# Attention of a conv/attention hybrid in 64-token chunks with two heads on the partitions, softmax sums on TensorE

## Chip, cores, metric

One core of a Trainium2 chip runs the whole program. The metric is the device time of one execution in microseconds; the time before is the median of three runs. A time within 0.2% of it cannot be told from no change.

## The reference

Input x is [16, 128, 64, 64] (16 images, 128 channels, 4096 tokens each). Layer 0 is a selective-scan (Mamba-like) block with a residual; layer 1 is an attention whose score doesn't depend on a query token, and then a routed feed-forward. The change is in the attention:

```python
def _L1_attn_ref(x, W_kv, q_proj):            # x: layer-normed tokens [16, 4096, 128], 8 heads of 128
    kv = jnp.einsum('btd,ed->bte', x, W_kv).reshape(b, t, h, d, 2)
    kv = jax.nn.silu(kv)
    k, v = (kv[..., 0], kv[..., 1])
    s = jnp.einsum('hd,bthd->bth', q_proj, k)          # one score per token and head
    m_A = jax.lax.cummax(s, axis=1)                    # running maximum over the tokens
    exp_scores = jnp.exp(s - m_A)
    u_A = jnp.cumsum(exp_scores, axis=1)               # running sum
    w_A = jnp.cumsum(exp_scores[..., None] * v, axis=1)
    output = w_A / u_A[..., None]
    return output.mean(axis=2)                         # mean over the heads
```

So each token's output is a mean over heads of a weighted running sum of all values so far. Kernels before and after get exp(s) once per token, write the weight of token s in the output of token t as exp(s_s - m_s - log u_t), and keep the sum over finished chunks as a carry.

## The kernel before

The program has three parts: the fused scan and attention, the routing, and the feed-forward with its write-back. The change lies in the first, which runs from the start to about 9590 us.

Work goes in blocks of 512 tokens (`L`), 8 per image, 128 in all. The outer loop runs over k; in round k the scan works on block k (`cur`), ends block k-1 (`prev`: gate, output projection) and prepares block k+1 (`nxt`: convolution, `xproj`, `delta`), while the attention works on block k-9 (`m`), ends block k-10 (`mp_`) and norms block k-8 (`mn`). The first nine rounds have no attention, 119 have both, and the last ten have attention alone. The inner loop runs over n = 0 to 15, the states of the scan: DVE multiplies (`bx`) and scans (`h`, two halves), POOL multiplies by C (`da`), PE adds it up in `y_ps` (`add_y`, called from `sums_of_y`), and ACT makes the decays exp(delta A) eight states ahead (`decays`, each decay two activations of 128x512 written to `da`). Between these, `beside(n)` places the pieces of the attention, convolution and projections, written out by hand; `between(n)` stands between the two half scans on DVE.

All five engines run in program order: every call goes through the class `InOrder`, so in the profile these instructions all carry line 31 and are told apart by their tiles. An instruction that waits therefore holds up everything written after it on its engine; transfers are issued by SP, ACT and POOL in the same order. PSUM gives three banks in turn to nearly all products (`bank`, pool `ps`), one to `acc` (the scores `s_ps` or the attention's sums `ao_ps`), and the rest to `y_ps` and `bx`.

The attention of a block, in order:
- `ln_center` to `ln_apply`: layer norm; DVE writes `xn` at n = 14 from `rstd`, which ACT makes at n = 10.
- `key` (8 heads, n = 0 to 2): a product of 512 columns and a SiLU on ACT each (`k_ps`, `kt`).
- `score` (n = 1 and 3): 8 heads x 4 chunks of 128 tokens, weights of 32 columns, into `s_ps`, whose row 32j+5g+c holds chunk c of head 4g+j.
- `score_max`, `score_less` (n = 4), `score_exp`, `score_sum` (n = 6), with `from_chunks` for what the earlier chunks hand over: running maximum and sum by scans on DVE, exp and logarithm on ACT.
- `score_log`, `rest`, `split`, `store_parts` (n = 7), `spread_parts` (n = 10, SP): scores and logarithms are split in three bf16 parts, written to DRAM, and read back as rows of `lh` and `rh`, so that a product gives the log weights.
- `inverse` (n = 7): `e`, the factor 1/u for the carry; `turn_weights` (n = 8): exp(s) transposed into `e1`.
- `value` (n = 8, 9 for the first half, n = 3 of the next round for the second): 4 chunks x 2 products of 512 columns.
- `weights`, `attend`, `carry_on`, `attend_before`: per chunk of 128 tokens the log weights and the mask by products in `w_ps`, two exps on ACT (`wm`), 8 products of 128x128 into `ao_ps` (channel-major), 8 small ones for the carry, a copy of the carry on ACT. Chunks 0 and 1 at n = 11 to 14, chunks 2 and 3 at n = 4 to 8 of the next round.
- `add_x`, `finish`: the residual by a product with the identity, a scaled copy and a store, each for half a block.

Of the kernel before, what the change touches and what calls it, by code (L numbers as in the profile page):

```python
# [8 lines left out]
F32 = mybir.dt.float32  # L9
# [6 lines left out]
P = 128  # L16
# [23 lines left out]
def conv_attn_hybrid(ctx: ExitStack, tc: tile.TileContext, x, w_in, conv_w, conv_b, w_xproj, w_dt, b_dt,  # L40
# [6 lines left out]
    NCH = T // P  # L47
    DI = w_in.shape[1] // 2
# [32 lines left out]
    with ExitStack() as st:  # L81
# [10 lines left out]
        identb = [wp.tile([P, P], BF16, name=f"identb{u}") for u in range(2)]  # L92
        nc.vector.tensor_copy(identb[0], ident)
        for u in range(2):
            nc.vector.tensor_copy(identb[1][:, bass.ts(u, 64)], ident[:, bass.ts(1 - u, 64)])
        minusb = wp.tile([P, P], BF16, name="minusb")
        nc.vector.tensor_scalar(minusb, ident, -1.0, None, ALU.mult)
        ident_hd = wp.tile([P, P], F32, name="ident_hd")
        nc.vector.tensor_scalar(ident_hd, ident, float(HD), None, ALU.mult)

        maskb = [wp.tile([P, P], BF16, name=f"maskb{u}") for u in range(2)]
# [21 lines left out]
        q1 = wp.tile([P, 4, 2, CB, 32], F32, name="q1")  # L123
        e1 = wp.tile([P, CB * 4, 2, 32], F32, name="e1")

        lh = wp.tile([P, L], BF16, name="lh")  # L130
        rh = wp.tile([P, 4, L], BF16, name="rh")
        off = wp.tile([P, CB], F32, name="off")
        carry = wp.tile([P, L // P, P], F32, name="carry")
        negc = wp.tile([P, 1], F32, name="negc")
        zs = {what: [wp.tile([P, 32], F32, name=f"z_{what}{a}") for a in range(2)] for what in ("max", "sum")}
        for z in (*zs["max"], *zs["sum"]):
            nc.gpsimd.memset(z, 0.0)
        nc.vector.memset(negc, NEG)
        nc.vector.memset(q1, 0.0)
        nc.vector.memset(e1, 0.0)  # L140
        nc.vector.memset(carry, 0.0)
        nc.vector.memset(lh, 0.0)
        for u in range(2):
            rows = slice(64 * u, 64 * u + 64)
            nc.vector.tensor_reduce(negc[rows, :], ident[rows, 64 * u + 12 : 64 * u + 15], mybir.AxisListType.X, ALU.add)
        nc.vector.tensor_scalar(lh, lh, negc, None, ALU.subtract)
        nc.vector.memset(rh, 0.0)
        for x in range(4):
            for u in range(2):
                rows = slice(64 * u, 64 * u + 64)  # L150
                nc.vector.tensor_reduce(negc[rows, :], ident[rows, 64 * u + 3 * x : 64 * u + 3 * x + 3],
                                        mybir.AxisListType.X, ALU.add)
            nc.vector.tensor_scalar(rh[:, x, :], rh[:, x, :], negc, None, ALU.subtract)
        for c in range(CB):
            nc.vector.tensor_reduce(negc, ident.rearrange("p (j r) -> p r j", r=32)[:, c : c + 6 : 5, :],
                                    mybir.AxisListType.XY, ALU.add)
            nc.vector.tensor_scalar(off[:, c : c + 1], negc, 1.0, -OFF, ALU.subtract, ALU.mult)
# [12 lines left out]
        with tc.tile_pool(name="prep", bufs=1) as prep:  # L170
            mask = prep.tile([P, P], F32, name="mask")
            nc.gpsimd.memset(mask, 0.0)
            nc.gpsimd.affine_select(out=mask, in_=mask, compare_op=ALU.is_ge, fill=OFF, base=0,
                                    pattern=[[1, P]], channel_multiplier=-1)
            nc.vector.tensor_copy(maskb[0], mask)
            mask_ps = ps.tile([P, L], F32, tag="ps", name="mask_ps")
            nc.tensor.matmul(mask_ps[:, :P], identb[1], maskb[0], start=True, stop=True)
            nc.vector.tensor_copy(maskb[1], mask_ps[:, :P])
# [10 lines left out]
            for g in range(2):  # L189
                for c in range(CB):  # L190
                    nc.vector.tensor_copy(q1[:, :, g, c, 5 * g + c], qt_ps[:, 4 * g : 4 * g + 4])
# [18 lines left out]
        vp_ = st.enter_context(tc.tile_pool(name="vp", bufs=2))  # L210
# [278 lines left out]
        def score(m, g):  # L489
# [5 lines left out]
            for c in range(CB):  # L495
                for j in range(4):
                    PE.matmul(s["s"][32 * j : 32 * j + 32, :P], q1[:, j, g, c, :], kt[j][:, bass.ts(c, P)],
                              start=(g == 0 and c == 0), stop=(g == 1 and c == CB - 1))

        def from_chunks(m, what, local, first, op0, op1, data):  # L500

            b, i = divmod(m, NBLK)
            last = stp.tile([P, 32], F32, tag=f"last_{what}", name=f"last_{what}")
            DVE.transpose(last, local[:, P - 32 :])
            z = zs[what][m % 2]
            if i == 0:
                DVE.memset(z[:, 0:10:5], first)
            else:  # L510
                DVE.tensor_reduce(z[:, 0:10:5], gn[b][what][:, 4:14:5].unsqueeze(2), mybir.AxisListType.X, ALU.max)
            gn[b][what] = z
            for g in range(2):
                DVE.tensor_tensor_scan(z[:, 5 * g + 1 : 5 * g + 5], bc(data[:, 0:1], [P, CB]),
                                       last[:, 5 * g : 5 * g + 4], z[:, 5 * g : 5 * g + 1], op0, op1)
            back = stp.tile([P, 32], F32, tag=f"back_{what}", name=f"back_{what}")
            DVE.transpose(back, z)
            return back[:, 31:32]

# [76 lines left out]
        def value(m, c, g):  # L596
            s = att[m]
            if g == 0:
                s["v", c] = vp_.tile([P, HD, P], F32, tag="v", name="v")
# [65 lines left out]

# [556 lines left out]
```

## Time and profile before

| what | before |
|---|---|
| time of the runs | 10512.2 us median (10492.8, 10512.2, 10512.5) |
| profiled execution: span | 10498.7 us |
| profiled execution: its own time | not recorded; the span lies among the runs, 13.5 us under their median |
| fused scan and attention, last xn | 9587.7 us |
| xn to xn, a common block with scan and attention | 71.7 us |
| granted TensorE clock, mean | 0.941 |

A line of the profile names the line, the engine, the operation, the tiles as out<-in with partitions x elements, and xcount. In groups there follow the busy time, the mean ns of one, and the idle time just before with what ended it. In the timeline a line has the start and the duration in us, and merged instructions of a kind are one line with their number; in brackets stands the idle time before it with what ended it. PE's f32 products are two records each (bf16 ones and transposes one). The duration of a PE record includes the pipeline, so the cost of a group is the distance to the next group's start.

### The profile page before, as it was taken

The numbers are of one execution on the slowest core, as the hardware profiler recorded it, in microseconds if no ns is written. First come the engines' busy times: TensorE is split into PE (matmuls) and PEld (weight loads), VectorE is DVE, ScalarE is ACT, GpSimd is POOL, SyncE is SP. The second block draws the span as 40 slices with busy tenths as digits, with TensorE's granted clock in tenths as the row PEclk, the third lists the DMA queues.
The fourth block names the chain that finished last, engine by engine and source line by source line (L and its number), as shares of the span: only waits on it lengthen the run. The fifth ranks groups of instructions, "written<-read, shape, count | busy, mean of one in ns | idle before, by whom it ended". The sixth has DMA issues, their size and how long they took to land.

```text
span 10498.7 us, 163128 instructions
## 1 busy us (share of the span) xinstructions
PE 9306.2 (89%) x58461; PEld 5584.4 (53%) x58461; DVE 8947.7 (85%) x9987; ACT 7317.3 (70%) x12924; POOL 7411.9 (71%) x4387
## 2 busy tenths in 40 slices
PE   5689999999999999999999999999999999988775
PEld 3345555555555555555555555555555555545652
DVE  8999999999999999999999999999999999911743
ACT  5567777777777777777777777777777777755740
POOL 7887787878788777878787877788787878810000
PEclk7789999999999999999999999999999999998886
DMA  6676767676676667676766666676666667611358
GB/s 174 174 189 168 184 167 184 170 179 173 166 186 165 183 168 184 169 185 169 179 175 163 189 163 185 169 184 170 182 169 174 180 164 181 166 45 42 114 163 344
DMA packets 889083, 1794.65 MB, mean 171 GB/s; under 512 B 96896, under 2 KB 182544, under 8 KB 881104
## 3 DMA queue, kind: packets, MB, share of 16 engines
q1 hardware_dynamic: 732912, 1414.88, 48.0%
q0 software_dynamic: 73728, 268.47, 12.9%
q10 hardware_dynamic: 81632, 100.88, 3.0%
q8 instruction: 462, 7.57, 0.3%
q14 instruction: 349, 2.86, 0.1%
HBM read 1363.98 MB, written 151.52 MB: 144 GB/s over the span
## 4 chain that ended last, share of the span: by engine, by line
PE 46%; DVE 23%; ACT 18%; issue 9%; DMA 4%; ACTq 1%; SPq 0%; POOL 0%; DVEq 0%; POOLq 0%
DVE h L31 11%; DVE bx L31 8%; ACT da L31 7%; PE ao_ps L31 6%; PE y_ps L31 6%; PE v_ps L31 5%; PE xs_ps L31 4%; PE o_ps L31 4%; PE carry_ps L31 3%; PE k_ps L31 3%; PE dt_ps L31 2%; PE dbl_ps L31 2%; PE z_ps L31 2%; PE w_ps L31 2%; ACT wm L31 2%
## 5 line engine op out<-in xcount | busy, mean ns | idle before, releaser
L31 POOL TENSOR_TENSOR da<-h,bct 128x1024 f32<-128x1024 f32 x2048 | 6599.6, 3223 | 1718.2 <-DVE h L31 643.0
L31 DVE TENSOR_TENSOR_SCAN h<-da,state,bx 128x512 f32<-128x512 f32 x3584 | 4414.8, 1265 | 169.7 <-DVE bx L31 2.4
L31 DVE TENSOR_TENSOR bx<-du,bct 128x1024 f32<-128x1024 f32 x2048 | 2608.0, 1273 | 261.9 <-DMA bct<-bcs 195.0
L31 ACT ACTIVATE da<-delta,a_neg 128x512 f32<-128x512 f32 x4096 | 2603.0, 718 | 35.7 <-DMA da<-da 30.6
L31 PE MATMUL y_ps<-ident,da 128*128 128x128 f32 x12288 | 1773.8, 297 | 203.5 <-POOL da L31 103.8
L31 PEld LDWEIGHTS y_ps<-ident,da 128*128 128x128 f32 x12288 | 1534.0, 153 | 629.2 <-issue 372.6
L31 PE MATMUL v_ps<-wv,xn 128*128 128x512 f32 x2048 | 1031.5, 625 | 207.2 <-ACT xc L31 193.8
L31 PE MATMUL xs_ps<-xb,wc 128*128 128x512 f32 x2048 | 987.9, 620 | 141.3 <-DVE z L31 139.5
L31 PEld LDWEIGHTS ao_ps<-wm,v 128*128 128x128 f32 x8192 | 980.3, 193 | 244.2 <-issue 153.4
L31 ACT ACTIVATE v<-v_ps 128x512 f32<-128x512 f32 x1024 | 612.5, 600 | 681.6 <-PE v_ps L31 653.1
L31 PE MATMUL ao_ps<-wm,v 128*128 128x128 f32 x8192 | 1027.8, 279 | 54.7 <-ACT wm L31 45.3
L31 PE MATMUL k_ps<-xn,wk 128*128 128x512 f32 x2048 | 943.3, 594 | 0.0
L31 ACT ACTIVATE kt<-k_ps 128x512 f32<-128x512 f32 x1024 | 587.2, 600 | 207.6 <-PE k_ps L31 185.6
L31 PEld LDWEIGHTS v_ps<-wv,xn 128*128 128x128 f32 x2048 | 317.0, 188 | 758.6 <-ACT v L31 251.1
L31 ACT ACTIVATE wm<-w_ps 128x512 f32<-128x512 f32 x1024 | 555.9, 595 | 203.9 <-PE w_ps L31 197.8
L31 PEld LDWEIGHTS xs_ps<-xb,wc 128*128 128x128 f32 x2048 | 375.0, 198 | 567.4 <-issue 379.2
L31 DVE TENSOR_TENSOR_SCAN h<-da,bx 128x512 f32<-128x512 f32 x512 | 600.0, 1207 | 25.8 <-ACT w L31 0.5
L31 PEld LDWEIGHTS k_ps<-xn,wk 128*128 128x128 f32 x2048 | 370.3, 191 | 319.1 <-issue 253.1
L31 POOL COPY state<-h 128x2 f32<-128x2 f32 x1792 | 525.0, 293 | 0.0
L31 POOL DMA_DIRECT2D da<-da x512 | 449.9, 879 | 92.0 <-POOL state L31 52.6
L31 ACT ACT_TABLE_LOAD x395 | 506.8, 1283 | 9.9 <-issue 3.5
L31 ACT COPY carry<-carry_ps 128x128 f32<-128x128 f32 x512 | 133.6, 261 | 539.3 <-PE carry_ps L31 539.3
(196 smaller groups left out, 10678.1 us busy)
## 6 DMA issues: line engine op xcount, KB each, us to landing
bct<-bcs SPq DMA_DIRECT2D x2048, 512.0 KB
da<-da POOLq DMA_DIRECT2D x512, 512.0 KB, 7.8
xs<-t_d SPq DMA_DIRECT2D x240, 256.0 KB
xs<-in_x_dram SPq DMA_DIRECT2D x128, 256.0 KB
xt<-in_x_dram SPq DMA_DIRECT2D x64, 512.0 KB
t_d<-xt SPq DMA_DIRECT2D x64, 512.0 KB
t_d<-xs ACTq DMA_DIRECT2D x256, 128.0 KB
t<-t_d SPq DMA_DIRECT2D x128, 256.0 KB
```

What stands on the lines that cost most here:

```text
L31: return lambda *args, **kw: self.tc.keep_in_program_order(f(*args, **kw))
```

## The change

- Chunks have 64 tokens instead of 128, eight to a block; `s_ps` is 128 rows of 64 columns (row 32j+16g+c).
- Two heads stand on the partitions of a chunk: `value` makes the values of heads 0 to 3 on partitions 0 to 63 and of heads 4 to 7 on 64 to 127, in two products of 64 rows.
- `weights` handles four chunks in one call: one bf16 product of 94 rows and 256 columns per chunk holds log weights and mask together; 2 exps per call.
- `attend` has the weights as stationary operand: outputs are token-major (`o`, 64 tokens at a time), four products per chunk, each for two heads. The chunks' sums for the carry go to the third 128 columns of the same bank.
- `take_sums`, `carry_on`, `attend_before`: the sums are copied once per half block, and products with constant triangles (`below`, `final`) turn them into the carry before each chunk, in the bank's last 128 columns; that is copied too.
- `take_o`, `turn_o`, `finish`: the result is copied with its scale, transposed by PE into a bank of the pool `ps`, the residual added there, copied out and stored.
- The running sum isn't scanned on DVE: `turn_scores` and `score_sum` make it by products on PE (`wt`, `tri`, `below`, `final`), with the chunk's total from `score_exp`'s accumulator; only the running maximum goes over the chunks on DVE.
- `inverse` makes eight activations of 64 columns and moves from n = 7 to n = 11; `spread_scores` (for `e1`) moves to n = 6.
- `store_parts` writes rows of 64 elements, `spread_parts` issues 10 transfers instead of 16.

The diff, with the setup of constants and the old bodies (shown above) left out. The functions:

```diff
         def score(m, g):
...
             kt = [s.pop(("kt", 4 * g + j)) for j in range(4)]
+            for c in range(NC8):
+                r = 16 * g + c
                 for j in range(4):
+                    PE.matmul(s["s"][32 * j : 32 * j + 32, :64], q1[:, 4 * g + j, 31 - r : 63 - r],
+                              kt[j][:, bass.ts(c, 64)], start=(g == 0 and c == 0), stop=(g == 1 and c == NC8 - 1))
+        def score_max(m):
+            s = att[m]
+            s["mx"] = a1.tile([P, 64], F32, tag="mx", name="mx")
+            DVE.tensor_tensor_scan(s["mx"], bc(negc, [P, 64]), s["s"][:, :64], NEG, ALU.max, ALU.max)
+        def score_less(m):
+            i = m % NBLK
+            s = att[m]
+            mx, z = s.pop("mx"), zl[m % 2]
+            DVE.transpose(z[:, 32:], mx[:, 32:])
+            if i == 0:
+                DVE.memset(z[:, 0:48:47], NEG)
+            else:
+                DVE.tensor_reduce(z[:, 0:48:47], zl[1 - m % 2][:, NC8 : NC8 + 17 : 16].unsqueeze(2), mybir.AxisListType.X,
+                                  ALU.max)
+            DVE.tensor_tensor_scan(z[:, 1:25], open_, z[:, 32:56], z[:, 0:1], ALU.min, ALU.max)
+            back = stp.tile([P, 32], F32, tag="back", name="back")
+            DVE.transpose(back, z[:, :32])
+            s["x2"] = a1.tile([P, 2, 64], F32, tag="x2", name="x2")
+            DVE.scalar_tensor_tensor(s["x2"][:, 0, :], mx, back[:, 31:32], s["s"][:, :64], ALU.max, ALU.subtract)
+        def score_exp(m):
+            s = att[m]
+            s["tot"] = stp.tile([P, 1], F32, tag="tot", name="tot")
+            s["w"] = a1.tile([P, 64], F32, tag="w", name="w")
+            ACT.activation(s["w"], s["x2"][:, 0, :], AF.Exp, scale=-1.0, accum_out=s["tot"])
+        def turn_scores(m):
+            s = att[m]
+            et = s["et"] = bank("et_ps")
+            w = s.pop("w")
+            for u in range(2):
+                PE.matmul(et[64 * u : 64 * u + 64, :P], w, ident, start=True, stop=True)
+            s["wt"] = a1.tile([64, P], F32, tag="wt", name="wt")
+            ACT.copy(s["wt"], et[:64, :P])
+        def spread_scores(m):
+            et = att[m].pop("et")
+            for u in range(2):
+                rows = slice(64 * u, 64 * u + 64)
+                src = et[rows, :P].rearrange("p (j g r) -> p g r j", j=4, g=2)[:, u, :NC8, :]
+                dst = e1[rows].rearrange("p (c k) -> p c k", k=P + 1)[:, :, 16 * u : P : 32]
+                ACT.copy(dst, src)
+        def score_sum(m):
             b, i = divmod(m, NBLK)
+            s = att[m]
+            u = s["u"] = bank("u_ps")
+            PE.matmul(u[:, :64], s.pop("wt"), tri[:64, :64], start=True, stop=False)
+            PE.matmul(u[:, :64], below, bc(s.pop("tot"), [P, 64]), start=False, stop=(i == 0))
+            if i:
+                PE.matmul(u[:, :64], final[NC8 - 1], bc(gn[b].pop("sum"), [P, 64]), start=False, stop=True)
         def score_log(m):
             s = att[m]
+            u = s.pop("u")
+            ACT.activation(s["x2"][:, 1, :], u[:, :64], AF.Ln, bias=tiny)
+            last = gn[m // NBLK]["sum"] = stp.tile([P, 1], F32, tag="last", name="last")
+            ACT.copy(last, u[:, 63:64])
+            s["parts"] = a1.tile([P, 3, 2, 64], BF16, tag="parts", name="parts")
+            ACT.copy(s["parts"][:, 0], s["x2"])
         def inverse(m):
             s = att[m]
+            s["e"] = a1.tile([P, NC8, 64], F32, tag="e", name="e", bufs=2)
+            for c in range(NC8):
+                ACT.activation(s["e"][:, c], s["x2"][:, 1, :], AF.Exp, bias=off[:, c : c + 1], scale=-1.0)
...
         def store_parts(m):
             s = att[m]
+            s["pd"] = bcd.tile([3, 2, P, 64], BF16, tag="pd", name="pd")
+            ACT.dma_start(s["pd"].rearrange("t w p s -> p (t w) s"), s.pop("parts").rearrange("p t w s -> p (t w) s"))
         def spread_parts(m):
+            pd = att[m].pop("pd")
             for u in range(2):
+                for x in range(HD // 2):
+                    row, of = 64 + 12 * u + 3 * x, 32 * x + 16 * u
+                    SP.dma_start(lh[row : row + 3, :, u, :], pd[:, 0, of : of + NC8, :])
+                row = 88 + 3 * u
+                SP.dma_start(rh[row : row + 3].rearrange("t x c s -> t x (c s)"),
+                             pd[:, 1].rearrange("t (x r) s -> t x (r s)", r=32)[:, :, 16 * u * 64 : 16 * u * 64 + L])
+        def value(m, c):
+            s = att[m]
+            vp = bank("v_ps")
             for u in range(2):
+                PE.matmul(vp[64 * u : 64 * u + 64, :], s["xn"][:, bass.ts(c, 64)],
+                          wv[:, bass.ts(u, 4), :].rearrange("p h d -> p (h d)"), start=True, stop=True)
+            v = s["v", c] = vp_.tile([P, 4, P], F32, tag="v", name="v")
+            ACT.activation(v.rearrange("p x d -> p (x d)"), vp, AF.Silu)
+        def weights(m, f):
+            s = att[m]
+            wm = s["wm"] = a1.tile([P, CB, 4, 64], F32, tag="wm", name="wm", bufs=2)
+            for q in range(2):
+                rp = bank("w_ps")
+                for a in range(2):
+                    c = CB * f + 2 * q + a
+                    PE.matmul(rp[:, bass.ts(a, L // 2)].rearrange("p (x t) -> p x t", t=64),
+                              lh[:94, c].rearrange("p u s -> p (u s)"), rh[:94, :, c, :], start=True, stop=True,
+                              skip_group_check=True)
+                ACT.activation(wm[:, bass.ts(q, 2)].rearrange("p c x t -> p (c x t)"), rp, AF.Exp)
+        def attend(m, f, q):
+            s = att[m]
+            if q == 0:
+                s["o"] = acc.tile([P, 4, P], F32, tag="acc", name="ao_ps")
+            o, wm = s["o"], s["wm"]
+            v = [s.pop(("v", CB * f + 2 * q + a)) for a in range(2)]
+            for x in range(4):
+                for a in range(2):
+                    PE.matmul(o[64 * a : 64 * a + 64, q, :], wm[:, 2 * q + a, x, :], v[a][:, x, :],
+                              start=(q == 0 and x == 0), stop=False, skip_group_check=True)
+            for a in range(2):
+                c = CB * f + 2 * q + a
                 for j in range(4):
+                    PE.matmul(o[32 * j : 32 * j + 32, 2, :], e1[:, c * P + 32 * j : c * P + 32 * j + 32], v[a][:, j, :],
+                              start=False, stop=(q == 1 and a == 1), skip_group_check=True)
+        def take_sums(m):
+            s = att[m]
+            s["sums"] = a1.tile([P, P], F32, tag="sums", name="sums")
+            ACT.copy(s["sums"], s["o"][:, 2, :])
+        def carry_on(m, f):
+            b, i = divmod(m, NBLK)
+            s = att[m]
+            first = i == 0 and f == 0
+            PE.matmul(s["o"][:, 3, :], below, s.pop("sums"), start=False, stop=first, skip_group_check=True)
             if not first:
+                PE.matmul(s["o"][:, 3, :], final[NC8], gn[b]["carry"], start=False, stop=True, skip_group_check=True)
+            gn[b]["carry"] = a1.tile([P, P], F32, tag="carry", name="carry", bufs=2)
+            ACT.copy(gn[b]["carry"], s["o"][:, 3, :])
+        def attend_before(m, f):
+            s = att[m]
+            for q in range(2):
+                c = CB * f + 2 * q
+                PE.matmul(s["o"][:, q, :], s["e"][:, c : c + 2, :].rearrange("p a t -> p (a t)"), gn[m // NBLK]["carry"],
+                          start=False, stop=True, skip_group_check=True)
+        def take_o(m):
+            s = att[m]
+            s["ot"] = short("ot")
+            ACT.activation(s["ot"][:, : 2 * P], s.pop("o")[:, :2, :].rearrange("p q d -> p (q d)"), AF.Copy, scale=1.0 / HD)
+        def turn_o(m, f):
+            s = att[m]
+            s["to"] = bank("to_ps")
+            ot = s.pop("ot")
+            for q in range(2):
+                PE.matmul(s["to"][:, bass.ts(q, P)], ot[:, bass.ts(q, P)], ident, start=(q == 0), stop=False,
+                          is_transpose=True, skip_group_check=True)
+            PE.matmul(s["to"][:, : 2 * P], ident, s["x"][:, bass.ts(f, 2 * P)], start=False, stop=True,
                       skip_group_check=True)
+        def finish(m, f):
             b, i = divmod(m, NBLK)
+            s = att[m] if f == 0 else att.pop(m)
+            xs = s["x"][:, bass.ts(f, 2 * P)]
+            ACT.copy(xs, s.pop("to")[:, : 2 * P])
+            ACT.dma_start(t2_d[b, :, i * L + f * (L // 2) : i * L + (f + 1) * (L // 2)], xs)
```

Their places in the order, in `beside` (guards and unchanged pieces of other blocks cut; the `decays` lines stay):

```diff
 n == 0:
-    attend_before(mp_, 1); add_x(mp_, 0)
+    turn_o(mp_, 0)
     key(m, 0), key(m, 1), key(m, 2)
     finish(mp_, 0)
...
 n == 3:
     score(m, 1)
-    for x in range(4, 8): value(mp_, x // 2, x % 2)
+    for c in range(CB): value(mp_, CB + c)
 n == 4:
     score_max(m)
-    weights(mp_, 2)
+    weights(mp_, 1)
     conv(nxt, 0)
 n == 5:
-    attend(mp_, 2)
+    attend(mp_, 1, 0)
     score_exp(m)
     decays(k, n, 2)
-    carry_on(mp_, 2); attend_before(mp_, 2)
+    attend(mp_, 1, 1); take_sums(mp_)
 n == 6:
-    weights(mp_, 3)
+    turn_scores(m)
     out_proj(prev)
-    attend(mp_, 3)
+    carry_on(mp_, 1); score_sum(m); spread_scores(m)
     decays(k, n, 2)
     put_back(prev)
-    carry_on(mp_, 3)
 n == 7:
     score_log(m)
+    attend_before(mp_, 1)
     rest(m, 1)
+    take_o(mp_)
     split(m, 1)
     conv(nxt, 1, range(KC // 2))
     decays(k, n, 2)
     rest(m, 2); split(m, 2); store_parts(m)
-    inverse(m)
     conv(nxt, 1, range(KC // 2, KC)); conv_silu(nxt)
 n == 8:
-    attend_before(mp_, 3); add_x(mp_, 1)
+    turn_o(mp_, 1)
     finish(mp_, 1)
-    turn_weights(m); value(m, 0, 0)
+    value(m, 0)
     xproj(nxt); store_bc(nxt)
-    value(m, 0, 1)
+    value(m, 1)
 n == 9:
-    value(m, 1, 0), value(m, 1, 1)
+    value(m, 2), value(m, 3)
 n == 11:
     weights(m, 0)
+    inverse(m)
     decays(k, n, 2)
 n == 12:
-    attend(m, 0); attend_before(m, 0)
+    attend(m, 0, 0)
     decays(k, n, 2)
-    carry_on(m, 0)
 n == 13:
-    weights(m, 1)
+    attend(m, 0, 1)
     decays(k, n, 2)
+    take_sums(m)
 n == 14:
     ln_apply(mn)
-    attend(m, 1)
+    carry_on(m, 0)
     decays(k, n, 2)
-    carry_on(m, 1)
+    attend_before(m, 0)
 n == 15:
+    take_o(m)
     decays(k, n, 2)
```

In `between(n)` the call `score_less(m)` at n = 4 stays, and `score_sum(m)` at n = 6 goes.

## Prediction

> **What bounds the kernel now.** I read the busy shares of the page first:
>
> ```profile
> PE 9306.2 (89%) x58461; PEld 5584.4 (53%) x58461; DVE 8947.7 (85%) x9987; ACT 7317.3 (70%) x12924; POOL 7411.9 (71%) x4387
> PE 46%; DVE 23%; ACT 18%; issue 9%; DMA 4%; ACTq 1%; SPq 0%; POOL 0%; DVEq 0%; POOLq 0%
> ```
>
> The second line, the chain that ended last, changes engine all the time, so no busy share decides alone. I took one block (512 tokens) out of the steady stretch and read DVE in the timeline:
>
> ```profile
> 3000.21 0.69 DVE L31 TENSOR_TENSOR xn<-cen_ps,rstd 128x512 f32<-128x512 f32 x1 [1.27 <-ACT rstd L31]
> 3026.21 0.41 DVE L31 TENSOR_TENSOR_SCAN mx<-negc,s_ps 128x128 f32<-128x128 f32 x1
> 3031.32 0.68 DVE L31 TENSOR_TENSOR z<-yb_ps,z 128x512 f32<-128x512 f32 x1
> 3071.94 0.69 DVE L31 TENSOR_TENSOR xn<-cen_ps,rstd 128x512 f32<-128x512 f32 x1 [1.28 <-ACT rstd L31]
> ```
>
> From xn to xn is 71.7 us; that is the common period, and over the steady blocks the mean is 72.3. I cut it in two. Stage A runs from xn to the end of the second gate (z, 3032.0): 31.8 us, DVE without a gap. Stage B runs from there to the next xn: 39.9 us, which ends in a wait for rstd, so PE and ACT set it. How near ACT and PE are to setting stage A too is seen in their timelines:
>
> ```profile
> 3000.82 1.09 ACT L31 ACTIVATE wm<-w_ps 128x512 f32<-128x512 f32 x2 [0.65 <-PE w_ps L31]
> 3001.79 5.01 ACT L31 ACTIVATE da<-delta,a_neg 128x512 f32<-128x512 f32 x8
> 3006.70 0.25 ACT L31 COPY carry<-carry_ps 128x128 f32<-128x128 f32 x1
> 3006.84 1.08 ACT L31 ACTIVATE wm<-w_ps 128x512 f32<-128x512 f32 x2
> 3007.81 3.79 ACT L31 ACTIVATE da<-delta,a_neg 128x512 f32<-128x512 f32 x6
> 3013.00 1.28 ACT L31 ACT_TABLE_LOAD   x1
> 3014.30 1.09 ACT L31 ACTIVATE kt<-k_ps 128x512 f32<-128x512 f32 x2
> 3052.68 1.28 ACT L31 ACTIVATE e<-x,off 128x128 f32<-128x128 f32 x4 [0.41 <-ACT parts L31]
> ```
>
> ```profile
> 3003.53 0.65 PE L31 MATMUL carry_ps<-v,e 128*32 128x128 f32 x16
> 3012.82 2.74 PE L31 MATMUL k_ps<-xn,wk 128*128 128x512 f32 x6
> 3018.08 1.08 PE L31 MATMUL s_ps<-kt,q 128*32 128x128 f32 x32
> 3032.06 3.70 PE L31 MATMUL xs_ps<-xb,wc 128*128 128x512 f32 x8 [1.37 <-DVE z L31]
> ```
>
> ACT has no gap from wm to the first kt (3000.8 to 14.3). The last score product ends at 3025.45, and DVE takes it (mx) at 3026.21: stage A has 0.76 us to spare. PE waits 1.37 us for the gate before the convolution. A change that lengthens the scores' way by more than 0.8 us moves the period.
>
> **Work removed and added, per block.** DVE loses the sum's scan, two transposes, two 4-step scans and a reduce ((144.3+27.1+27.1+46.0+12.9)/128 = 2.0 us) and 0.3 on halved ones: 2.3 of 67.4 busy. PE: the weights' product drops from 5.3 ((295.9+219.2+159.9)/128) to about 1. The weighted sums have as many records, but 64 columns wide, two side by side. The nearest row, pl (128*64), issues 16 records in 1.03 us where ao needs 1.87, so 8.0 falls to 4.1. The values become 32 records of half width instead of 16. If the halves share the array as pl's do, they cost the same; if not, 16 x 0.43 = 6.9 more. I take the first plus 0.1 per lone call (0 to 0.43, a lag of one record). The scores have 128 records of 64 columns instead of 64 of 128: 16 records of this width took 0.58 us (3003.53 to the next product at 3004.11), 32 took 1.01 (3018.08 to 3019.09), so 27 ns a record and 0.15 for the group. If time followed columns, a score call would stay at 1.0; if records set it, 64 x 27 + 150 ns = 1.9. I take 1.9, since the record of M=32 also brings its own weight load. New small products (turned scores, sums, turned outputs) add 2, rest loses 0.5. PE loses some 5 us in all, and ACT comes out even: four wm of 0.49 go, and half-size exps of e (8 for 4), two take_o of 0.35, two copies and an accumulator read come.
>
> The Trainium skill (TensorE: Matmul & The Clock Gate, "Wait — 56ns, not 53.3ns?") has a rule against halving the columns: starts of products never come closer than about 25 ns however few columns they have. By it a score call is 64 x 25 ns + 150 = 1.75 us, an estimate from that page, and the sum below would be 0.3 us a block smaller.
>
> **Where it lies: stage A, T = 0 at the end of rstd (3000.17).** ACT now has inverse in front of the decays: four e of 128 columns took 1.28, so 0.32 each; da of 512 takes 0.61, hence 0.76 ns a column and 0.27 for 64 columns, 8 x 0.27 = 2.15 (half of 0.32 would make 1.3). So: wm until 1.4, inverse 3.55, then 12 da of 0.613 (n = 11 to 13) 10.9, and only then take_sums 11.1, since ACT keeps program order. PE has done both attends by about 6 and waits some 5 us in carry_on; queued behind it are y, attend_before, turn_o and the keys. carry_on (4 records of 0.117) and hand-offs 11.75, ACT's carry copy 12.1, two da 13.3, take_o 13.7, two da 14.95, table 16.25, kt0 16.85 (before: 14.7). turn_o holds one of three banks until finish, which comes after three kt, so the third key waits for kt0 and ends at 17.75; after one y the fourth key starts at 18.6, before at 16.1 (3016.27): +2.5. Two score calls add 0.9 each. The last score ends at 29.6 instead of 25.3, and mx starts at 29.7 instead of 26.04. From there to the second gate's end DVE needs 5.5 (5.79 less the halved work): stage A ends at 35.2 instead of 31.8, **+3.4**. What PE saved is spent waiting for ACT.
>
> **Stage B, t = 0 at the gate's end.** Convolution 3.55, y 4.4, both attends (2 x 1.6) 7.6, turn_scores 0.35, out_proj 3.5: 11.45 (before 12.7). PE's carry_on stands behind out_proj, and ACT's carry copy waits for it with spread_scores, four da, put_back and the logarithm queued behind; before, those da lay beside out_proj. So carry_on 11.9, copy 12.25, spread 12.65, da 15.1, put_back 16.15, Ln, last and parts 17.05, take_o and split 17.7, da 20.15, split and DMA issue 20.9, table 22.2, xc 22.9; before 23.9. e has gone from here (-1.3), but the logarithm comes later than before. From xc to rstd, PE's row of v, dbl, z and dt stays at 16.0, plus 0.3 for the halves. **-0.7**.
>
> What stays at nothing: DVE's 2.3 us, because it then waits at mx and at xn; if stage A were DVE's again, 0.3 of it would count there. spread_parts issues 10 DMAs instead of 16 on SP (0.33 us apart, -2.0), so the bct loads behind it come earlier. That shortens bx's wait for bct, which already lies ahead of the longer wait for rstd. store_parts now writes 768 rows of 128 B: its queue's mean is 3.0% x 10499 x 16 / 81632 = 62 ns a packet, so 768/16 x 62 ns = 3 us at most later, while in another block spread_parts ends at 5160.6 and the first reader starts at 5169.99. If that cover failed, the 3 us would go on stage B. The setup's extra memsets and copies are some 5 us.
>
> **The clock.** Where PE had idled 1.38 us before the convolution, the granted clock was 0.72 in one block (5128 to 5134), and its 8 records took 5.23 us to the next product instead of 3.54 at clock 1.00; about a third of the blocks have a stage B of 41.4 to 41.8 for 39.7. The new 5 us idle will meet this more often; what runs cold first has slack towards kt0. I take +0.5 a block, bounds 0 and 2. The same page of the skill ("What's actually happening") states half rate after an idle window of about 3.4 us and full rate after as long a busy one; by it the first 3.4 us after the idle would cost up to 1.7 us a block, an estimate, 200 us in all.
>
> **Sum.** 119 blocks have scans and attention: (3.4 - 0.7) x 119 = +321; clock +60. The last ten have attention alone at about 47 us each (PE-bound, without the decays that delay ACT): PE's saving of 5 less new hand-offs, -4 x 10 = -40 (0 to -60). Together +341 on the span of 10498.7. Around the span lie 13.5 us if the profiled execution was like the median, 10512.2, of runs from 10492.8 to 10512.5. That makes 10853, rounded to **10850 us**.
>
> **Rivals.** *Cost follows columns* (faster): if 64-column instructions cost half of 128-column ones, the scores add nothing (-1.8) and inverse is 1.3 (-0.85). A is then +0.75, and Ln, parts and splits take 0.4 off B, now -1.1: (0.75 - 1.1) x 119 - 40 = -82, so 10430. Records overlap four deep in s_ps now, which speaks for it; the row of 224 ns for a 64-column ACT copy against 261 for 128 speaks against. It decides once they cost less than about 65%. If ACT's order also held PE less than walked and DVE ended A again at 31.5, it would be (-0.3 - 1.1) x 119 - 40 = -207, 10305. Chance 0.24. *No change*: the added and the saved cancel within 0.2%, 21 us, about what a measurement of this kernel can tell: 0.06. *Halves don't share* (slower still): values +6.9, half in each stage, on PE's chain: 10850 + 821 = 11670; pl speaks against: 0.04. The forecast, own range 10600 to 11150: 0.66.
>
> **Numbers.** The range 10290 to 11150 leaves out about 1 in 10 on either side. Faster 0.24, same 0.06, slower 0.70.
>
> **What would show it.** Right: DVE waits at mx for s_ps; PE's longest wait in a block is carry_on's on sums; the first kt comes 16 to 17 us after rstd; a score group lasts about 1.9 us; xn to xn is about 74.5 us. Wrong: mx doesn't wait and the period is under 71.7, a score group lasts 1 us, or v_ps records don't overlap.

## The result, and the profile after

| | before | after |
|---|---|---|
| time of the runs, median | 10512.35 us (10492.82 to 10518.95) | 10687.16 us (10675.27 to 10696.04) |
| ratio, 95% interval | | 1.017 [1.0155, 1.0184] |
| profiled execution: span | 10498.7 us | 10694.3 us (its own time 10696.04) |
| mean granted TensorE clock | 0.941 | 0.908 |
| first xn / last xn | 617.2 / 9587.7 us | 620.9 / 9789.4 us |
| stage A, mean (median) of the steady blocks | 31.74 (31.80) us | 35.45 (35.44) us |
| stage B, mean (median) | 40.55 (39.75) us | 38.91 (38.35) us |
| xn to xn, mean (median) | 72.29 (71.63) us | 74.35 (74.20) us |
| xn to xn in the last blocks, attention alone | 46.8 us | 41.3 us |

The steady blocks are 109 of the 119 with scan and attention. Slower by 174.8 us, where +338 was forecast: the sign and the stage were right, the size was twice too large. The sum closes on the profiled spans: (74.35 - 72.29) x 119 = +245, ten last blocks at 41.3 instead of 46.8 = -55, and +3.7 before the first xn, together +194; the spans differ by 195.6.

Busy shares, the chain that ended last, and two groups of the page after (busy us, mean ns of one; then the idle time ahead of them and what ended it):

```profile
PE 9085.2 (85%) x68316; PEld 5489.8 (51%) x68316; DVE 8651.8 (81%) x9089; ACT 7241.1 (68%) x13564; POOL 7371.6 (69%) x4412
PE 58%; ACT 26%; DVE 9%; issue 3%; DMA 3%; ACTq 0%; POOL 0%; SPq 0%; DVEq 0%; POOLq 0%
L31 PE MATMUL ao_ps<-sums,below 128*128 128x128 f32 x512 | 135.2, 351 | 465.9 <-ACT sums L31 465.8
L31 ACT ACTIVATE kt<-k_ps 128x512 f32<-128x512 f32 x1024 | 600.8, 601 | 470.1 <-PE k_ps L31 460.3
```

Every engine is busy for less time than before, and yet the program is longer: DVE has lost 296 us and fallen from 23% of the chain to 9%, PE and ACT carry 84% of it. The two groups show how they hold each other up: PE stands 466 us before `carry_on`, waiting for ACT's copy of the sums, and ACT stands 460 us before the keys' SiLU, waiting for PE.

DVE in one block (timeline: start, duration, and in brackets the idle time ahead):

```profile
3068.95 0.69 DVE L31 TENSOR_TENSOR xn<-cen_ps,rstd 128x512 f32<-128x512 f32 x1 [3.90 <-ACT rstd L31]
3099.42 0.29 DVE L31 TENSOR_TENSOR_SCAN mx<-negc,s_ps 128x64 f32<-128x64 f32 x1 [1.68 <-PE s_ps L31]
3104.40 0.68 DVE L31 TENSOR_TENSOR z<-yb_ps,z 128x512 f32<-128x512 f32 x1
3143.43 0.69 DVE L31 TENSOR_TENSOR xn<-cen_ps,rstd 128x512 f32<-128x512 f32 x1 [1.66 <-ACT rstd L31]
```

The wait that was forecast is there: `mx` now waits for `s_ps`, and stage A (here 3068.95 to 3105.08, 36.1 us; 35.45 in the mean) is no longer DVE's. (The block shown is the first of an image, so the two records that carry the sums on from the block before are missing in it.) Who sets it can be read off the chain of waits in the same window (start, duration, what; count):

```profile
3070.09 2.01 ACT e L31 x8
3072.10 7.35 ACT da L31 x12
3079.45 0.16 ACT sums L31
3079.66 0.81 PE ao_ps L31 x2
3080.49 0.28 ACT carry L31
3080.81 1.22 PE ao_ps L31 x4
3082.03 3.41 PE y_ps L31 x16
3085.44 1.23 PE to_ps L31 x4
3086.68 2.67 PE k_ps L31 x6
3098.32 1.07 PE s_ps L31 x64
3099.42 0.06 DVE mx L31
```

Up to `sums` it is the walk of the prediction: inverse (2.01 us), twelve decays, then the copy, while PE waits. After `carry` it isn't: PE gets through 16 records of y in 3.41 us, 16 for which it needed 1.75 in a block of before:

```profile
3010.41 1.91 PE L31 MATMUL y_ps<-ident,da 128*128 128x128 f32 x16
3012.16 0.39 PE L31 MATMUL ao_ps<-e,carry 128*128 128x128 f32 x2
```

The same stretch of the kernel after in the table by windows says why (stretch and its length; busy us and count of PE, PEld, DVE, ACT, POOL; granted clock; DMA share; GB/s):

```profile
3074.50:3079.60 5.10, 1.15 (x15) 0.86 (x8) 4.93 (x5) 5.10 (x10) 3.73 (x3) 1.00 0.52 90
3079.60:3081.80 2.20, 1.79 (x6) 1.49 (x7) 2.17 (x3) 1.32 (x4) 1.87 (x3) 0.52 0.08 29
3081.80:3085.20 3.40, 3.40 (x18) 3.40 (x17) 3.27 (x3) 3.08 (x5) 3.40 (x2) 0.50 0.70 143
3085.20:3086.60 1.40, 1.40 (x7) 1.22 (x6) 1.37 (x2) 0.00 (x0) 1.08 (x2) 0.54 0.25 75
3086.60:3090.00 3.40, 3.40 (x15) 1.74 (x14) 3.23 (x4) 1.81 (x4) 3.23 (x4) 1.00 0.45 137
```

PE is idle for 4.0 us of the first row; then the clock is granted at half for some 7 us, all of it on the path to the first key. In the third row PE is busy for the whole stretch, and a reader who looks at busy shares alone takes it for the bound.

### The profile page after: what moved, and what is told of

Read it like the earlier page. It is cut to its first block, busy times and chain, and to the rows that moved or that the text cites. A ratio compares the mean times of both kernels' runs of the same rounds, so it can differ in the third digit from the quotient of the medians.

```text
span 10694.3 us, 180670 instructions
## 1 busy us (share of the span) xinstructions
PE 9085.2 (85%) x68316; PEld 5489.8 (51%) x68316; DVE 8651.8 (81%) x9089; ACT 7241.1 (68%) x13564; POOL 7371.6 (69%) x4412
## 4 chain that ended last, share of the span: by engine, by line
PE 58%; ACT 26%; DVE 9%; issue 3%; DMA 3%; ACTq 0%; POOL 0%; SPq 0%; DVEq 0%; POOLq 0%
ACT da L31 13%; PE y_ps L31 11%; PE k_ps L31 8%; PE ao_ps L31 7%; PE v_ps L31 5%; PE xs_ps L31 5%; PE o_ps L31 4%; DVE h L31 4%; PE s_ps L31 3%; ACT e L31 3%; PE dt_ps L31 3%; DVE bx L31 2%; PE z_ps L31 2%; PE dbl_ps L31 2%; ACT L31 1%
## 5 line engine op out<-in xcount | busy, mean ns | idle before, releaser
L31 DVE TENSOR_TENSOR bx<-du,bct 128x1024 f32<-128x1024 f32 x2048 | 2555.5, 1248 | 152.5 <-DMA bct<-bcs 82.7
L31 PE MATMUL y_ps<-ident,da 128*128 128x128 f32 x12288 | 1991.3, 321 | 202.9 <-DMA da<-da 101.8
L31 PEld LDWEIGHTS y_ps<-ident,da 128*128 128x128 f32 x12288 | 1760.2, 169 | 600.3 <-issue 324.7
L31 PE MATMUL v_ps<-wv,xn 128*64 128x512 f32 x4096 | 1092.2, 607 | 26.8 <-ACT xc L31 26.3
L31 PE MATMUL ao_ps<-v,wm 128*64 128x128 f32 x8192 | 573.6, 283 | 27.2 <-ACT wm L31 27.2
L31 PEld LDWEIGHTS v_ps<-wv,xn 128*64 128x64 f32 x4096 | 259.3, 135 | 575.9 <-ACT v L31 174.6
L31 PE MATMUL ao_ps<-sums,below 128*128 128x128 f32 x512 | 135.2, 351 | 465.9 <-ACT sums L31 465.8
L31 PEld LDWEIGHTS ao_ps<-v,wm 128*64 128x64 f32 x8192 | 447.9, 139 | 122.5 <-issue 52.2
L31 DVE TENSOR_TENSOR xn<-cen_ps,rstd 128x512 f32<-128x512 f32 x128 | 88.5, 691 | 507.5 <-ACT rstd L31 472.9
L31 ACT COPY carry<-ao_ps 128x128 f32<-128x128 f32 x256 | 68.2, 266 | 576.8 <-PE ao_ps L31 576.8
```

The source lines that it names most:

```text
L31: return lambda *args, **kw: self.tc.keep_in_program_order(f(*args, **kw))
```

## The experiments

Two theories were open. *Cold clock*: stage A is late because PE idles before `carry_on` and then runs at half speed. *Order alone*: it is late by ACT's queue and by PE's dependent steps, and the clock matters little, as the prediction had it (+0.5 us a block). All ratios are against the kernel before; the kernel after stands at 1.017.

**e1, the sums ahead of two decays.** ACT's copy of the sums moves in front of one `decays` call.

```diff
 n == 13:
     attend(m, 0, 1)
-    decays(k, n, 2)
     take_sums(m)
+    decays(k, n, 2)
```

> The changed kernel with take_sums(m) moved in front of the two decays of n = 13. Theory 'ACT's order and the clock': take_sums comes 2.45 us earlier, carry_on with it; the one idle stretch of PE of about 4 us is cut in two (the carry copy still stands behind the decays), PE keeps its full clock, the first kt is ACT's at 16 us after rstd instead of PE's at 18.6. Stage A falls by about 2, so 119 x 2 = 240 us less than the changed kernel: ratio to the kernel before about 0.994 instead of 1.017. Rival 'more and smaller records load PE': the order on ACT doesn't matter, ratio stays at 1.015 to 1.019. Rival 'ACT's work sets stage A': ACT has as much to do as ever, ratio 1.010 or more.

Measured: 10532.21 us, 1.0023 [1.0013, 1.0032]. `sums` comes at 7.83 us after xn instead of 10.44, the first key at 16.75 instead of 17.92, stage A is 34.25. One line moved is worth 155 us, less than the 240 expected: the clock record of its trace still has half rate in stage A of all 109 steady blocks, for 3.4 us in 73 of them and for 6.8 us in 36. That PE's wait for ACT sets the stage is shown; the two theories are not parted, since a shorter wait is also a warmer clock (in the kernel after, 56 blocks have 3.4 us and 53 have 6.8).

**e2, inverse back at n = 7.** Undoes that one move of the change.

```diff
 n == 7:
     store_parts(m)
+    inverse(m)
 n == 11:
     weights(m, 0)
-    inverse(m)
```

> The changed kernel with inverse(m) moved back from n = 11 to n = 7, behind store_parts. Theory 'ACT's order and the clock': the eight e (2.0 us) leave the front of stage A, the sums come 2.0 us earlier, PE idles 2 us less and keeps its clock for most of the time; stage A falls by 2.5 to 3.5, stage B grows by up to 2.0 as the e stand before the convolution's table load. Net -0.5 to -1.5 a block, ratio 1.000 to 1.011, with A under 33.5 and B about 40. Rival 'more and smaller records load PE': no change of A, B +2.0, ratio 1.035 or more.

Measured: 10819.17 us, 1.0295 [1.028, 1.0311]: slower than the kernel after, and outside what was expected. Stage A fell nearly as walked (35.45 to 33.08), but stage B rose by 3.4 (38.91 to 42.29). `e` itself takes 2.0 us in front of `xc`. The rest is in the timeline and the windows of PE:

```profile
3080.74 1.45 PE L31 MATMUL v_ps<-wv,xn 128*64 128x512 f32 x4 [2.29 <-ACT xc L31]
3081.97 2.77 PE L31 MATMUL dbl_ps<-xc,wx 128*40 128x512 f32 x3
```

```profile
3080.70:3082.70 2.00, 1.96 (x5) 0.53 (x6) 1.97 (x2) 1.30 (x3) 1.66 (x3) 0.65 0.18 53
3082.70:3084.50 1.80, 1.80 (x4) 0.48 (x4) 1.67 (x3) 0.12 (x1) 1.80 (x1) 0.50 0.15 41
3084.50:3086.50 2.00, 2.00 (x7) 0.67 (x4) 1.97 (x2) 0.84 (x2) 1.61 (x3) 0.94 0.89 147
```

PE now stands 2.29 us before the values, and runs cold after it: from the first value to `var_ps` it takes 9.9 us (3080.74 to 3090.65), in the kernel after 8.2 (3127.71 to 3135.93). So the change's move of inverse was right by 1.0 us a block, and the expectation failed on the term that failed in the prediction, the clock after a wait.

**e3, PE kept busy.** Four products whose output nobody reads, in front of PE's wait.

```diff
 n == 13:
     attend(m, 0, 1)
+    idle = bank("idle_ps")
+    for j in range(4):
+        PE.matmul(idle, wk[:, j, :], att[m]["xn"], start=True, stop=True)
     decays(k, n, 2)
```

> The changed kernel with four products of 512 columns, whose result nobody reads, put on PE behind attend(m, 0, 1), in the stretch in which PE waits for ACT's sums (3.4 us of work in a gap of about 4). Theory 'clock': PE does more work and the program gets faster, since y, turn_o and the first keys then run at the full clock; the first kt comes at 16 to 16.5 us after rstd instead of 18.6, stage A falls by 1.5 to 2.4, that is 180 to 290 us less, with some 30 us added in the ten blocks without a scan: ratio 0.992 to 1.003. If the wait alone counts and the clock doesn't: ratio 1.017 to 1.021. If PE's load counts: +3.4 x 119 = 400 us, ratio 1.055.

Measured: 10446.29 us, 0.9941 [0.9926, 0.9956]. PE does 474 us more work, and the program is 241 us shorter than the kernel after. The timeline of PE:

```profile
3068.76 3.70 PE L31 MATMUL idle_ps<-xn,wk 128*128 128x512 f32 x8
3074.39 0.49 PE L31 MATMUL ao_ps<-sums,below 128*128 128x128 f32 x2 [1.05 <-ACT sums L31]
3076.01 1.91 PE L31 MATMUL y_ps<-ident,da 128*128 128x128 f32 x16
3078.41 2.83 PE L31 MATMUL k_ps<-xn,wk 128*128 128x512 f32 x6
```

and the windows over its first and its later steps:

```profile
3074.30:3076.00 1.70, 1.25 (x8) 1.06 (x9) 1.70 (x2) 0.90 (x4) 1.70 (x1) 1.00 0.17 66
3076.00:3078.40 2.40, 2.40 (x22) 2.36 (x21) 2.23 (x3) 2.38 (x6) 2.07 (x3) 1.00 0.21 75
```

`sums` comes no earlier to speak of (10.29 us after xn for 10.44), ACT's order is untouched, and PE's steps from y to the first key take 2.40 us at clock 1.00 where the block of the kernel after took 4.69 (3081.82 to 3086.51). Stage A is 33.14, and in none of the 109 steady blocks is there any half rate left in it. ACT's work and order are the same; what differs is the clock (and that the filler takes a bank in its turn, which e9, below, rules out as the cause). The cold clock is worth 2.3 us a block, and *order alone* falls.

**e9, half the filling.** Two of those products instead of four (`range(2)`).

> The changed kernel with two instead of four unread products of 512 columns in PE's idle stretch of stage A, so that about 2 us of idle are left. If the clock falls only after an idle of more than 3 us, this is worth as much as four products (ratio 0.993 to 0.998, with less added in the ten blocks without a scan); if an idle of 2 us is often enough, about half or less is won: ratio 1.002 to 1.012.

Measured: 10510.53 us, 1.0003 [0.9989, 1.0018], its runs spread from 10486 to 10543, against 10444 to 10456 in e3. That is neither of the two outcomes expected: about three quarters of what e3 won. In the block that I read PE still waits 2.47 us for `sums` and is at clock 1.00:

```profile
3037.91 0.49 PE L31 MATMUL ao_ps<-sums,below 128*128 128x128 f32 x2 [2.47 <-ACT sums L31]
```

The program's mean clock is 0.928, between the two others (0.908 and 0.946), and its steady blocks can be sorted by the half rate that the clock record has in their stage A: 80 have none, and stage A takes 33.32 us in the mean; 22 have 3.4 us of it, and take 35.16; 7 have 6.8 us, and take 36.35. This is one program with one order and the same banks, so these 2 to 3 us go with the clock and not with the filler or its bank. A wait of some 2.5 us sometimes costs the clock and sometimes not; the last section says when.

**e4, DVE's saving given back.** Two scans of 128 columns more on DVE at n = 6, 2.25 us a block, whose output nobody reads.

```diff
+                if m is not None and n == 6:
+                    for a in range(2):
+                        DVE.tensor_tensor_scan(spare, bc(ones[:, 0:1], [P, P]), ident, 0.0, ALU.mult, ALU.add)
```

> The changed kernel with DVE's removed load put back as two scans of 128x128 between the half scans of n = 6 (1.13 us each, from constants, unread). Theory: DVE waits 3 to 4 us at xn in stage B, so these 2.25 us cost nothing: ratio 1.016 to 1.019. Rival 'DVE sets the time and its saved work was worth something': +2.25 x 119 = 270 us, ratio 1.042.

Measured: 10700.23 us, 1.0182 [1.0167, 1.0197], its interval overlapping that of the kernel after. The DVE work that the change removes was worth nothing here.

**e5, stage A put in another order.** Both attends first, then inverse, the sums and the carry with no decay between; the turned outputs follow at n = 15 and no longer lie in front of the keys. The moves:

```diff
 n == 0:
-    turn_o(mp_, 0)
     key(m, 0), key(m, 1), key(m, 2)
-    finish(mp_, 0)
 n == 12:
     attend(m, 0, 0)
+    attend(m, 0, 1); inverse(m); take_sums(m); carry_on(m, 0)
     decays(k, n, 2)
 n == 13:
+    attend_before(m, 0)
     decays(k, n, 2)
 n == 14:
+    take_o(m)
     decays(k, n, 2)
 n == 15:
+    turn_o(m, 0); finish(m, 0)
```

(`inverse` goes from n = 11, `attend` and `take_sums` from 13, `carry_on` and `attend_before` from 14, `take_o` from 15.)

> The changed kernel with stage A's attention put in another order and nothing left out: both attends, inverse, take_sums and carry_on at n = 12 in front of its decays, attend_before at n = 13, take_o at n = 14, turn_o and finish at n = 15. Theory 'ACT's order and the clock': the sums are copied about 6 us after rstd instead of 10.4, PE has no idle stretch over about 2 us before the keys, kt0 comes at 16 to 16.5 instead of 17.9, and the third key needs no bank of kt0. Stage A falls from 35.4 to 32 to 33, 290 to 400 us less: ratio 0.980 to 0.990. Rival 'ACT's work sets stage A whatever the order': A 34 or more, ratio 1.005 or more.

Measured: 10414.43 us, 0.9914 [0.9899, 0.9929], a little above what was expected, with stage A at 33.21 instead of 32 to 33. `sums` comes at 5.16 us after xn, so the wait that the prediction named is down from 4.0 to 1.7 us; a second one, which nobody had walked, stands behind it: PE waits 2.46 us for `ot`, behind four decays on ACT, and then the clock goes (8 records of y in 1.71 us, from 3005.73 to 3007.44, and half rate for 3.4 us in 96 of the 109 steady blocks):

```profile
3005.00 0.44 PE L31 MATMUL to_ps<-ident,ot 128*128 128x128 f32 x2 [2.46 <-ACT ot L31]
```

**e6, stage B put in another order.** The carry and the running sum go ahead of the output projection on PE, and the logarithm ahead of four decays on ACT.

```diff
 n == 6:
     turn_scores(m)
-    out_proj(prev)
-    carry_on(mp_, 1); score_sum(m); spread_scores(m)
+    carry_on(mp_, 1); spread_scores(m); score_sum(m)
+    out_proj(prev)
+    score_log(m)
     decays(k, n, 2)
 n == 7:
-    score_log(m)
```

> The changed kernel with stage B's order changed: at n = 6 carry_on, spread_scores and score_sum stand in front of out_proj, and score_log in front of the decays of n = 6 (out_proj then has to wait for spread_scores to free a bank, about 1.3 us). Theory: ACT's copies, the logarithm and four decays lie beside out_proj instead of behind it, the convolution's SiLU comes 2 to 3 us earlier, stage B falls from 38.9 to 36 to 37.5: 170 to 340 us less, ratio 0.985 to 1.001. Rival 'PE's records set stage B': B stays within 0.7, ratio 1.010 or more.

Measured: 10444.02 us, 0.9935 [0.9919, 0.9952]; stage B 37.28 instead of 38.91, stage A nearly as it was (35.09). ACT's copy of the carry, first in the kernel after, then in e6:

```profile
3117.39 0.27 ACT L31 COPY carry<-ao_ps 128x128 f32<-128x128 f32 x1 [3.80 <-PE ao_ps L31]
```

```profile
3044.35 0.27 ACT L31 COPY carry<-ao_ps 128x128 f32<-128x128 f32 x1 [0.46 <-PE ao_ps L31]
```

The 3.8 us in which ACT stood behind `out_proj` are down to 0.46; stage B is 1.6 us shorter, half of that. With 0.4 from stage A it is 2.0 a block, and 243 us in all.

**e7, both orders; e8, both and `take_o` earlier.** e7 is e5 and e6 together. e8 takes away the second wait that e5 showed: `take_o` goes from n = 14 to n = 13, `turn_o` from 15 to 14.

```diff
 n == 13:
     attend_before(m, 0)
+    take_o(m)
     decays(k, n, 2)
 n == 14:
-    take_o(m)
+    turn_o(m, 0)
     decays(k, n, 2)
 n == 15:
-    turn_o(m, 0)
     finish(m, 0)
```

> Both orders together. Theory: the two gains add, since the stages follow each other: ratio 0.948 to 0.974, unless DVE (65 us of work a block) becomes the bound, which would be 65 x 119 us for the 119 blocks and a ratio of about 0.91. Rival: what is gained in A is lost in B because a faster stage lets PE idle and its clock drop at the next wait: ratio 0.98 or more.

> Both orders of e7, and in stage A take_o in front of the decays of n = 13 and turn_o at n = 14. In e7 PE still waits 2.5 us for ot in front of turn_o and then runs y and the keys at a low clock. Theory 'ACT's order and the clock': that idle stretch goes, the keys are ready when ACT is, stage A falls by 0.5 to 1.2, 60 to 140 us less than e7: ratio 0.950 to 0.959 instead of 0.964. Rival 'ACT alone sets the first kt by now': ratio 0.962 to 0.966.

Measured: e7 10128.76 us, 0.9641 [0.9626, 0.9655]; e8 10078.05 us, 0.9585 [0.9569, 0.9601]. In e7 the gains of e5 and e6 over the kernel after (0.0256 and 0.0235) add up, with 0.004 over, whose source I did not separate. In e8 stage A is 32.02 and stage B 37.18. Its DVE, and PE's steps from the carry to the keys:

```profile
3039.57 0.69 DVE L31 TENSOR_TENSOR xn<-cen_ps,rstd 128x512 f32<-128x512 f32 x1 [1.25 <-ACT rstd L31]
3065.88 0.29 DVE L31 TENSOR_TENSOR_SCAN mx<-negc,s_ps 128x64 f32<-128x64 f32 x1 [0.26 <-PE s_ps L31]
3107.62 0.69 DVE L31 TENSOR_TENSOR xn<-cen_ps,rstd 128x512 f32<-128x512 f32 x1 [1.63 <-ACT rstd L31]
```

```profile
3045.05 0.49 PE L31 MATMUL ao_ps<-sums,below 128*128 128x128 f32 x2 [1.68 <-ACT sums L31]
3048.84 0.44 PE L31 MATMUL to_ps<-ident,ot 128*128 128x128 f32 x2 [0.89 <-ACT ot L31]
3056.42 1.98 PE L31 MATMUL k_ps<-xn,wk 128*128 128x512 f32 x4 [1.51 <-ACT kt L31]
```

```profile
3051.30:3054.70 3.40, 3.40 (x16) 1.88 (x14) 3.23 (x3) 2.98 (x6) 3.10 (x3) 1.00 0.30 92
```

In these steps PE still waits three times, for 4.1 us in all, but never for more than 1.7 at once, and the clock stays at 1.00 where it was half. `mx` waits 0.26 us: stage A is nearly DVE's again. With the same operations as in the kernel after, in another order, the change makes the program 4.1% faster than before, not 1.7% slower.

## Why the prediction was right or wrong

**The sign and the wait: right.** DVE waits at `mx` for the scores (1.68 us); PE's longest wait in the block is `carry_on`'s on `sums` (4.01 us in the block shown, 465.9 us in all); xn to xn is 74.2 in a common block, 74.5 forecast. ACT's queue was walked well: inverse 2.01 us (2.15 taken), the copy of the sums done 10.7 us after xn (11.1 taken), the table load done 16.0 us after xn (16.25). But the first key starts 17.9 us after xn, not 16 to 17, and a score group of 1 us, which the prediction lists as a sign of being wrong, is what came.

**The score calls: wrong, 1.9 us taken, 1.03 measured.** The first 64 records start at 3091.87 and y follows at 3092.90:

```profile
3091.87 1.10 PE L31 MATMUL s_ps<-kt,q 128*32 128x64 f32 x64
3092.90 1.09 PE L31 MATMUL y_ps<-ident,da 128*128 128x128 f32 x8
```

So a record of 32 x 64 takes 16 ns in the mean, the same 1.0 us for a call as with half as many records twice as wide. The records start in fours 7 ns apart, a four every 56 ns; before, with 128 moving columns, a four came every 109 ns. The 27 ns a record that I built on came from groups with 128 moving columns; that records and not columns set the time was my choice between two bounds, and the other bound was right. The Trainium skill's figure (TensorE: Matmul & The Clock Gate, "Wait — 56ns, not 53.3ns?"), that starts never come closer than about 25 ns, does not hold for these records; the measurement decides. The step put 1.75 us too much on stage A.

**The clock: wrong in place and in size.** I had +0.5 us a block. In stage A it costs 2.3 (e3), and the step that named the cover ("what runs cold first has slack towards kt0") is the one that failed: the clock is half for some 7 us, not for the first few records, and the cold steps y, `to_ps` and keys lie on the path. The first key waits 2.60 us for `k_ps` although ACT's table had been ready since 3084.97:

```profile
3087.57 0.60 ACT L31 ACTIVATE kt<-k_ps 128x512 f32<-128x512 f32 x1 [2.60 <-PE k_ps L31]
```

In stage B it gave something back. Before, 31 of 109 blocks had a stage B over 41.1, 22 of them 41.3 to 41.8 (a fifth, not a third), for the common 39.7; I had read these as cold convolutions. For 17 of them that is right: their clock is 0.72 to 0.74 in the 6 us behind the gate, and their stage B 41.5 in the mean, which is 0.28 us a block over the 109. Another 13 lie eight blocks apart, in the rounds in which `gn_end` closes an image's group norm, mostly with a warm convolution; one is neither. After, these 13 rounds are the only ones above 41.1, and no convolution runs cold. So against the common block the clock costs 2.3 us in stage A and gives back about 0.3 in stage B, where I had +0.5.

Of the 147 us between +341 and +194, stage B accounts for 112, since its mean fell by 1.64 and not by 0.7; the last ten blocks for 15; stage A, 3.71 with its cold clock where I had 3.4 and 0.5, for 23; and the 3.7 before the first xn, which the sum left out, go the other way.

**Two errors that hid each other.** With the scores at 1.03 my walk gives 35.2 - 1.75 = 33.45 for stage A without a cold clock; e3, which is that case, has 33.14. The cold clock brings it to 35.45. So 35.2 was met by two wrong terms, which is luck, and the walk by itself was good to 0.3 us. The sign is luck too: with a warm clock the change would have stood at 0.9941 (e3), on the other side of no change. The wait that the prediction walked makes the program slower only through a cost that it had put at 0.5 us a block.

**Stage B: -0.7 forecast, -1.4 in a common block.** The end of the first half of `xc` came 22.5 us after the gate (22.9 taken, 23.9 before); that is 0.4. The other 0.3 is the charge for the values' halves, which do not cost it: 16 records of half width take 3.65 us (3099.28 to 3102.93), 8 of full width took 3.77. The halves share the array, as `pl` had suggested, and that rival falls.

**At nothing: right for DVE and the transfers.** e4 shows the 2.3 us of DVE to be worth nothing. PE waited 8.7 us in the whole program for the rows of `rh` (2.4 before), and DVE's wait for `bct` fell from 195.0 to 82.7 us, ahead of the longer wait for rstd. The last ten blocks gave -5.5 each (-4 taken), the setup +3.7 (some 5).

**The rivals.** *Cost follows columns* held for PE's score records, half the time for half the columns, and not for ACT: a 64-column `e` costs 0.25 us beside 0.32 for 128, 78% where that rival had half. Stage A rose by far more than the 0.75 us of that rival, for a reason that it did not contain.

## What to carry to other kernels

When an edit makes one engine wait for another inside a tight chain, walk the queue of the engine that is waited for, line by line, and then price what the waiting engine does just after: in this kernel TensorE's waits of 2.3 us (e2), 2.5 us (e5) and 4.0 us were followed by 3.4 to 6.8 us at half clock, on whatever came next. Where a stage turns out slower though every engine has less to do, look in the table by windows for a stretch with a busy PE and a clock of 0.5; filling the wait with unread products (e3) is the quick test, moving the awaited copy ahead of unrelated work (e1, e5, e6, e8) the cure. A smaller operation count is worth what the order lets through: the same operations gave 1.017 in one order and 0.9585 in another.

## What was not expected of the hardware

- The clock knows two values here, 1 and 0.5, and steps on a grid of 3.413 us that runs through the whole trace and takes no notice of the blocks (in the clock record of all eleven traces; other values in the tables by windows are mixtures). After 4.0 us without a product it was half for two steps, 6.8 us (3079.7 to 3086.5), though PE was busy for nearly all of them. After a wait of 2.29 us (e2) it was half for one step; after 2.47 us (e9) it stayed 1.00 in the block shown, and after 1.68 and 1.51 us (e8) too; after 1.38 us before, in the block that the prediction quotes, it was half for one step.
- What tells is how much of a step PE was busy, not the length of the wait alone. Between 1000 and 9000 us of the eleven traces there are 784 steps at full rate with PE busy for under 40%: a step at half rate followed every one of them. With 40 to 50% it followed 104 of 184, with over 80% none of 17976. From 50 to 80% the busy share does not tell: 68 of 2533 up to 70%, 921 of 1941 above that, and those, in the traces of before, after and e2, are mostly filled by `dt_ps`, products with 8 rows; whether such products count for less no run here shows. The wait in e2 lay within one step (first row, 33% busy), the one in e9 across two (second and third row, 51 and 66%):

```profile
3077.91:3081.32 3.41, 1.11 (x7) 0.33 (x7) 3.28 (x3) 3.39 (x8) 3.36 (x2) 1.00 0.24 57
3033.70:3037.10 3.40, 1.74 (x11) 0.97 (x9) 3.37 (x3) 3.40 (x7) 2.02 (x2) 1.00 0.51 117
3037.10:3040.50 3.40, 2.24 (x17) 2.05 (x18) 3.23 (x4) 2.82 (x7) 3.07 (x3) 1.00 0.14 42
```

- The Trainium skill (TensorE: Matmul & The Clock Gate, "What's actually happening") has half rate after an idle window of about 3.4 us, full rate after as long a busy one, and windows that run freely. The length and the free running agree with the grid of 3.413 us. By it two windows, 6.8 us, may pass before full rate, an estimate from that page; the 6.8 us after the 4.0 us wait agree with two, while the prediction had reckoned with one. That a window must be idle does not agree: one busy for 33% was enough in e2.
- More work made the program faster: 474 us of unread products on the engine that carries most of the chain took 241 us off.
- Product records with 32 weight columns and 64 moving columns in f32 start every 16 ns in the mean (64 in 1.03 us), in fours 7 ns apart.
